# Four transformer blocks on one core: new due times and margins in the build-time plan, normalisations on VectorE or ScalarE, and the fp4 constant inside the rounding

## The chip, the cores and the metric

The kernel runs on one core of a Trainium2 chip. The core has five engines that work side by side, each with its own queue: TensorE (PE; its weight loads are shown apart as PEld), VectorE (DVE), ScalarE (ACT), GpSimd (POOL) and SyncE (SP), which here issues all DMAs. An engine works through its queue in order, and waits on semaphores for what other engines produce. The metric is device time in microseconds; lower is better.

## The reference

The input is 8 sequences of 1024 rows by 256 columns, in float32. Four blocks follow each other, each with a layer normalisation in front and a residual sum behind. Cut to what matters:

```python
x = x + L0_attn(layernorm(x))   # flow-style linear attention, 16 heads of 16; inside it, layer norms
                                # and a GELU network 256 -> 1024 -> 256
x = x + L0_ffn(layernorm(x))    # relu(x @ w1 + b1) @ w2 + b2, width 1024
x = x + L1_attn(layernorm(x))   # softmax(Q K^T / 16) V, one head, within a sequence
x = x + L1_ffn(layernorm(x))    # fp4: silu(xq @ wgq.T) * (xq @ wuq.T), then quantised again @ wdq.T

def fp4_quant_dequant(x):       # blocks of 16 columns
    scale = max(abs(block)) / 6
    return nearest_on_grid([0, .5, 1, 1.5, 2, 3, 4, 6], abs(x / scale)) * sign(x) * scale
```

The first attention needs running sums along the rows of a sequence (of k, of q, of both weighted), so that a group of rows depends on the group before it. The softmax attention needs all 1024 rows of a sequence at once. The fp4 weights are 704 by 256 (gate, up) and 256 by 704 (down), and are quantised in the kernel.

## The kernel before, in words

**Tiling.** Rows go in chunks of 128 (64 chunks: 8 sequences of 8). Four chunks make a group of 512 rows, so there are 16 groups, two to a sequence; `p` numbers them. Two chunks of a group are a half.

**Stages.** They are written as Python generators:

- `linear_group(p)` normalises the four chunks (`front`), and then `linear_span` makes q and k, the running sums (`prod`, by VectorE's scan), the head sums on TensorE (`hsum`, narrow matmuls of 32 columns), and the weights per row. The first group is done in two halves (`near`). Through `spread` a packed row of weights goes to DRAM and back, widened.
- `linear_chunk(p, i)` makes v, the masked scores `sc` within a chunk (narrow `kz` matmuls), adds the running state `kv_sum`, projects with `wo`, normalises, and turns the result `h` into the half `hT`.
- `dense()` (L1412) runs the two 256-1024-256 networks for each half: 8 first matmul pairs into `hidden`, and 8 second ones that add into `acc`, two steps behind (`LAG`). `load_weights` fetches their weights again for each half pair, 256 KB in a DMA, two buffers each. `norms_1` and `norms_2` take the results, with layer normalisations, and turn them (`nT`, `n2T`).
- `soft_chunk(cc)` (L1580) does the softmax attention of a chunk and its fp4 network: scores, `prob` by Exp, `prob` turned into `probT`, product with `vt`, a normalisation `n`, `fp4(n)`, `n` turned into `xqT`, gate and up matmuls, `hid`, `fp4(hid)`, `hid` turned into `hqT`, the down matmul.
- `fp4_weights` quantises and turns 18 pieces of weights once; `softmax_weights` makes one matrix of Wq and Wk.

**Turning.** [...] rows must be transposed at many places. `flip` (L660) has two ways: on TensorE (two 128x128 matmuls against `ident`, a PSUM bank, one ScalarE copy), or by DMA: POOL copies the 32-bit tile as two halves of 16 bits (`cut`), a DMA transposes it (`spun`), and ScalarE copies it together. The first way is taken if `near` is asked for, or if `plan.idle` finds no part that could take TensorE now: `IDLE = 1, 0.0` (L29) means "fewer than one part for TensorE is ready, looking 0.0 us ahead".

**The plan.** The order of all instructions is made at build time by `Plan.run` (L313). Each generator (a part) yields a need: an engine, tiles that must be done, buffers or banks that must be free, a condition, and perhaps a due time `at`, counted in groups. The planner keeps its own clock for each engine, from a table of costs in `took` (L167), and takes the part with the smallest key:

```python
wait = max(max(t) - now - (0.3 if stays or part[2] < 0.0 else 0.0), 0.0)
unripe = 0.0 if urgent else max(t[1] + self.RIPE[queue] - now, 0.0)
key = wait, unripe, queue == "tensor", not stays, part[2]
```

`now` is TensorE's planned time. `unripe` is a margin: operands should have been done for `RIPE` us before a step is placed. `part[2]` is the due time, which decides last. For other engines than TensorE a step counts as startable 0.5 us before its engine is free (L288). All five queues are pinned: an instruction is chained to the one before it on its engine, so that the order of the plan is the order on the chip. If the plan sees TensorE pause for over 1.6 us ahead of one of its steps, `fill` (L1734) puts dummy matmuls of `ident` by `ident` there, one for each 0.22 us.

**Normalisation** (`layernorm`, L637): VectorE takes mean and variance, POOL makes `ln_ve` and `ln_rstd`, VectorE computes (x - mean) * rstd in one instruction.

**fp4** (L723): after scaling to blocks, ScalarE squares into `c` (bf16), a VectorE instruction adds 2^22 * 4/3 to `c`, and `src + c - c` rounds `src` to a step that grows with its size; then the block scale is multiplied on.

Of the kernel before, what the change touches and what calls it, by code (L numbers as in the profile page):

```python
# [17 lines left out]
P = 128  # L18
# [9 lines left out]
W_FF = 2  # L28
IDLE = 1, 0.0  # L29
RES = 10  # L30
HALVES = 5
LAG = 2
QB = 16
# [36 lines left out]
class Plan:  # L70
# [8 lines left out]

    RIPE = {"tensor": 1.0, "vector": 0.5, "scalar": 0.5, "gpsimd": 0.0, "sync": 3.0}  # L80
    SETS = {AF.Gelu: 1, AF.Exp: 2, AF.Sigmoid: 3}
# [177 lines left out]
    @staticmethod  # L259
    def need(queue, tiles, banks=0, when=None, at=None, unused=(), fresh=None, tiled=False):  # L260


        return SimpleNamespace(
            queue=queue, tiles=tiles, banks=banks, when=when, at=at, unused=unused, fresh=fresh,
            tiled=tiled,
        )

    def pe(self, *tiles, **kw):
# [14 lines left out]
    def ready(self, need):  # L283


        if need.when is not None and not need.when():
            return None
        free = self.free.get(need.queue, 0.0) - (0.0 if need.queue == "tensor" else 0.5)  # L288
        times = [0.0]
        times += [self.done.get(x.tensor.name, 0.0) for x in need.tiles]  # L290
        times += [self.used.get(x.tensor.name, 0.0) for x in need.unused]
        if need.banks:
            times.append(self.banks_free(need.banks))
        if need.fresh is not None:
            times.append(self.buffer(need.fresh)[0])
        return None if None in times else (free, max(times))
# [81 lines left out]
def block_stack_kernel(ctx: ExitStack, tc: tile.TileContext, a: dict, out: bass.AP):  # L378
# [258 lines left out]
    def layernorm(kind, src):  # L637
        mean, rstd = ln_stats(src)
        dst = yield from fresh(kind, dve(rstd), "n")
        nc.vector.tensor_scalar(dst, src, mean, rstd, ALU.subtract, ALU.mult)  # L640
        return dst
# [18 lines left out]
    def flip(src, dst, tiles=None, last=None, near=False):  # L660

        if not near:
            yield plan.pool(src)
            near = plan.idle(*IDLE)
        if near:
            yield pe(src, banks=1)
            bank = turned([src[:, k, :] for k in range(2)])
            if last is not None:
                plan.drop(last)
            if tiles is not None:  # L670
                tiles.cut += 1
            yield act(bank)
            nc.scalar.copy(dst, bank)
            if tiles is not None:
                tiles.done += 1
            return
        cut = yield from fresh("cut", plan.pool(src))
        nc.gpsimd.tensor_copy(
            cut.rearrange("p (h k t) -> p h k t", h=2, k=2),
            src.bitcast(U16).rearrange("p k (t h) -> p h k t", h=2),  # L680
        )
        if last is not None:
            plan.drop(last)
        if tiles is not None:
            tiles.cut += 1
        spun = yield from fresh("spun", dma(cut))
        nc.sync.dma_start_transpose(out=spun.rearrange("p (b t) -> p b t", t=P), in_=cut)
        plan.drop(cut)
        yield act(spun)
        nc.scalar.copy(  # L690
            dst.bitcast(U16).rearrange("p k (t h) -> p k t h", h=2),
            spun.rearrange("p (h k t) -> p k t h", h=2, k=2),
        )
        plan.drop(spun)
        if tiles is not None:
            tiles.done += 1
# [26 lines left out]
    def fp4(src, width, rows=P, factor=1.0):  # L723
# [21 lines left out]
            blocks(src, width),  # L745
            factor * (1.0 - 2.0**-23),
            wide(rc, rows, nb),
# [6 lines left out]
        yield dve(c)  # L754
        nc.vector.tensor_scalar(c, c, 2.0**22 * 4.0 / 3.0, None, ALU.add)
        nc.vector.tensor_tensor(src, src, c, ALU.add)
        yield dve(src)
        nc.vector.tensor_tensor(src, src, c, ALU.subtract)
        plan.drop(tile_c)
# [4 lines left out]
    def fp4_weights():  # L764
# [15 lines left out]
        for i, (src, turns) in enumerate(pieces):  # L780
            for j in range(i, min(i + 3, len(pieces))):
                if j not in raws:
                    ahead = pieces[j][0]
                    raws[j] = (yield from fresh(
                        "soft",
                        dma(at=2.0 + 2.5 * i / len(pieces), when=lambda: count["stage"] == 4),
                        "w_raw",
# [5 lines left out]
            raw = raws.pop(i)  # L793
            at = 2.0 + 2.5 * i / len(pieces)
            yield dve(raw, at=at)
# [179 lines left out]
    def linear_group(p):  # L975
# [28 lines left out]
        fronts = set()  # L1004
        yield dve(at=p, when=lambda: count["v"] == p * G)
        n0T = two(kept([P, 2 * GT], "n0T", 1))
        for i in range(G):
            plan.start(front(i), p + 0.03 * i - (p == 0 and i < 2))
        tiles = SimpleNamespace(
# [18 lines left out]
    def linear_span(p, span, fronts, tiles):  # L1028
# [16 lines left out]
        def turn(n):  # L1045
# [4 lines left out]
        yield pe(  # L1050
            at=p + 0.1 + after,
            when=lambda: fronts >= set(span)
# [24 lines left out]
        for n, pair in enumerate(((2, 0), (3, 1))):  # L1077
            for b in pair:
                need = dve(cur[b], at=p + 0.15 + 0.08 * n + after, when=turn("flow"))
                prod = prods[(b + 2) % 4] = (yield from fresh("flow", need, "prod"))[:, :width]  # L1080
                yield from running(prod, cur[b], past["cur"], b, opens, closes)
# [5 lines left out]
        ran.add(("flows", span.stop))  # L1087
        yield pe(*prods, banks=1, tiled=True, at=p + 0.3 + after, when=lambda: "hsum" in late)
        bank = head_sums(prods, span)
# [11 lines left out]
        for n, pair in enumerate(((2, 0), (3, 1))):  # L1101
            for b in pair:
                w = weighted[b]
                need = dve(w, at=p + 0.35 + 0.08 * n + after, when=turn("scale"))
                if near:
# [10 lines left out]
            for b in pair:  # L1116
# [3 lines left out]
                )  # L1120
        yield pe(*prods, banks=1, tiled=True, at=p + 0.5 + after, when=lambda: "positions" in late)
        bank = head_sums(prods, span)
# [62 lines left out]
        )  # L1185
        plan.start(scaled(), p + 0.55 + after)
        for i in span:
            plan.start(linear_chunk(p, i, n0T, comp, qk), p + 0.55 + 0.03 * i + after)

    def linear_chunk(p, i, n0T, comp, qk):  # L1190

        s, g = divmod(p, NG)
        past, c = seqs[s]["past"], p * G + i
        at = p - (p == 0 and i < 2)
        here = slice(i * P, (i + 1) * P)
# [40 lines left out]
        for e in range(2):  # L1236
# [5 lines left out]
                qk[1],  # L1242
                at=at + 0.62 + 0.06 * i,
                when=lambda: i in groups[p]["scaled"]
# [51 lines left out]
        if not end:  # L1296
            k_at = at + 0.66 + 0.06 * i
            need = plan.pool(at=k_at, when=lambda: count["attended"] >= c - (p > 0))
# [78 lines left out]
        if by_act and i == G - 1:  # L1377
            plan.drop(later)
        yield pe(xo, banks=1, at=at + 0.7 + 0.06 * i, when=lambda: "chunk" in late)
        bank = mm_bank()  # L1380
        for k in range(2):
# [12 lines left out]
            h,  # L1394
            at=at + 0.74 + 0.06 * i,
            when=lambda: half_fits(p, "hT", i // 2) and count["dense"] >= p - 1,
# [15 lines left out]
    def dense():  # L1412
# [4 lines left out]
        def second():  # L1417
# [21 lines left out]
            if f == NF - 1:  # L1439
# [10 lines left out]
                for j in range(2):  # L1450
                    norms = (norms_1, norms_2)[b]
                    plan.start(
                        norms(p, 2 * half + j, acc[:, j * D : (j + 1) * D], taken),
                        p + 1 + (2 * b + half + 1) / 4,
                    )

        def load_weights(names, used, loaded, first):

            ws, n = [], 0
            for p in range(flows):  # L1460
                for name in names:
                    for f in 2 * list(range(0, NF, 2)):
                        yield dma(
                            at=p + 0.9 + (2 * n % 32 + (0 if first else LAG)) / 32,
                            when=lambda: n < W_FF + used[0] // 2 and count["stage"] >= 2,
# [20 lines left out]
        for p in range(flows):  # L1486
            for b, (kind, ba, func) in enumerate((("hT", b1, AF.Gelu), ("nT", fb1, AF.Relu))):
                for half in range(2):
# [3 lines left out]
                    for f in range(NF):  # L1492
                        yield pe(
                            at=p + 1 + (16 * b + 8 * half + f) / 32,
                            when=lambda: n_turned.get((kind, half)) == 2 and w_in and "dense" in late,
# [84 lines left out]
    def soft_chunk(cc):  # L1580
# [3 lines left out]
        n2T, vt = q["n2T"], q["vt"]  # L1584
        at = 3.5 + min(cc, B * NCH - 10) / 4
        yield pe(
# [47 lines left out]
        for kb in range(NG):  # L1634
            tp = yield from fresh("prob", plan.pool(prob[kb], at=at + 0.25), "probT")
            probT.append(tp.rearrange("p (k t) -> p k t", k=G))
            rows_kb = prob[kb].rearrange("p (k t) -> p k t", k=G)
            flips.append(
                flip_all([(rows_kb[:, j : j + 2], probT[kb][:, j : j + 2]) for j in (0, 2)], at + 0.25)
            )  # L1640
# [23 lines left out]
        yield from fp4(n, D)  # L1664
        xqT = two((yield from fresh("soft", plan.pool(n, at=at + 0.5), "xqT")))
        yield from flip(two(n), xqT, last=n)
# [30 lines left out]
        for half in range(2):  # L1697
            tq = yield from fresh("prob", plan.pool(hid, at=at + 0.75), "hqT")
            hqT.append(tq.rearrange("p (k t) -> p k t", k=4))
        for j in range(0, len(INTER_TILES), 2):  # L1700
            src = two(hid[:, j * P : (j + 2) * P])
            pairs.append((src, hqT[j // 4][:, j % 4 : j % 4 + 2]))
        flips_h = flip_all(pairs, at + 0.75)
        yield plan.pool(when=lambda: flips_h.cut == len(pairs))
# [20 lines left out]
    def softmax_and_fp4():  # L1725
        for cc in range(B * NCH):
            q = seqs[cc // NCH]
            yield dve(
                at=3.5 + min(cc, B * NCH - 10) / 4,
                when=lambda: q["normed"] == NCH and cc - count["out"] < (8 if plan.spare else 4) and "softmax" in weights and "ends" in late,  # L1730
            )
            plan.start(soft_chunk(cc), 3.5 + min(cc, B * NCH - 10) / 4)

# [54 lines left out]
```

## Time and profile before

| What | Before |
|---|---|
| median of 3 runs | 2533.13 us (2532.2 to 2544.2) |
| the profiled execution's own time | 2542.89 us |
| its span, first to last instruction | 2541.2 us |
| mean granted TensorE clock | 0.995 |
| DMA traffic | 305.54 MB, mean 120 GB/s |
| DMA transposes (spun) | 713 |
| table loads on ScalarE | 166, 213.0 us |
| the chain that ended last | PE 67%, DVE 17%, DMA 6%, ACT 5%, POOL 3%, issue 2% |

Almost every instruction is recorded through one helper, so all carry line 359: groups are told apart by their tiles, written out<-in. A float32 matmul appears as two records (passes), a transposition as one. The busy time of a matmul is modelled [...], so records overlap; the distance from start to start says how long TensorE is taken.

### The profile page before, as it was taken

The page shows a single profiled execution, that of the slowest core. Times are in us where ns is not written, and L with a number is a line of the kernel's source. Part 1 is how long each engine was busy: PE and PEld are TensorE (multiplying, and loading weights), DVE is VectorE, ACT ScalarE, POOL GpSimd, SP SyncE. Part 2 cuts the span into 40 slices and gives each one's busy share as a digit, 9 for nine tenths or more (in the row PEclk, how much of TensorE's full clock was granted, in tenths as well). Part 3 has the DMA queues.
Part 4 walks back from the last instruction along what each step waited for, and adds up shares of the span by engine and source line. Part 5 has one row for each costly group of instructions (what it writes and reads, how often), then busy time and mean ns, then how long its engine had stood idle before and what let it go on. Part 6 is the DMA issues. An engine that isn't in the chain of part 4 may idle for free.

```text
span 2541.2 us, 47871 instructions
## 1 busy us (share of the span) xinstructions
PE 2469.1 (97%) x16713; PEld 1919.0 (76%) x16713; DVE 1995.0 (79%) x4414; ACT 1376.0 (54%) x2842; POOL 1089.1 (43%) x1947
## 2 busy tenths in 40 slices
PE   8999999999999999999999999999999999999999
PEld 7777777777777777777777777777677777877767
DVE  6786778877868778797987868787788887866788
ACT  4544556465565554556455464645656455545463
POOL 2343445452534525444452544635345353534242
PEclk9999999999999999999999999999999999999999
DMA  3445465565546544555545455555454645545342
GB/s 88 99 135 138 114 153 117 133 135 125 123 118 146 120 116 110 134 132 122 144 108 138 107 127 131 128 133 118 106 141 116 154 99 126 123 110 131 69 87 53
DMA packets 600977, 305.54 MB, mean 120 GB/s; under 512 B 404384, under 2 KB 589216, under 8 KB 600736
## 3 DMA queue, kind: packets, MB, share of 16 engines
q1 hardware_dynamic: 600736, 302.48, 49.6%
q8 instruction: 132, 2.16, 0.4%
q14 instruction: 109, 0.89, 0.1%
HBM read 188.17 MB, written 20.71 MB: 82 GB/s over the span
## 4 chain that ended last, share of the span: by engine, by line
PE 67%; DVE 17%; DMA 6%; ACT 5%; POOL 3%; issue 2%; SPq 1%; DVEq 0%; POOLq 0%; ACTq 0%
PE bank L359 67%; DMA spun<-cut 4%; DVE hid L359 2%; DVE n L359 2%; ACT L359 2%; DVE prod L359 2%; DVE ln_st L359 1%; DVE u L359 1%; POOL ln_rstd L359 1%; DMA spread<-packed 1%; DVE sc L359 1%; SPq L359 1%; DVE res L359 1%; DVE mx L359 1%; DVE ln_mv L359 1%
## 5 line engine op out<-in xcount | busy, mean ns | idle before, releaser
L359 PE MATMUL bank<-half,w_in 128*128 128x256 f32 x2048 | 532.2, 383 | 13.9 <-ACT half L359 9.9
L359 PE MATMUL bank<-w_out,hidden 128*128 128x256 f32 x2048 | 534.2, 385 | 8.7 <-DMA w_out<-in_L_ffn_w_dram 7.5
L359 PEld LDWEIGHTS bank<-w_out,hidden 128*128 128x128 f32 x2048 | 376.8, 191 | 108.9 <-issue 52.6
L359 PEld LDWEIGHTS bank<-half,w_in 128*128 128x128 f32 x2048 | 386.0, 191 | 88.5 <-issue 19.8
L359 POOL TENSOR_SCALAR ln_ve<-ln_mv 128x1 f32<-128x1 f32 x384 | 95.9, 250 | 737.6 <-DVE ln_mv L359 723.3
L359 POOL TENSOR_TENSOR ln_rstd<-ln_ve,neghalf 128x1 f32<-128x1 f32 x384 | 236.4, 616 | 31.9
L359 PE MATMUL bank<-n2T,qT 128*128 128x512 f32 x512 | 242.2, 595 | 4.3 <-ACT qT L359 3.6
L359 PE MATMUL bank<-vt,probT 128*128 128x256 f32 x1024 | 231.9, 379 | 0.0
L359 ACT ACT_TABLE_LOAD x166 | 213.0, 1283 | 16.2 <-DVE nmax L359 11.3
L359 ACT ACTIVATE hidden<-bank,c_L_ffn_b 128x256 f32<-128x256 f32 x256 | 121.0, 473 | 183.8 <-PE bank L359 182.9
L359 POOL COPY cut<-prob 128x512 uint16<-128x512 uint16 x211 | 143.2, 702 | 176.3 <-ACT prob L359 124.6
L359 PEld LDWEIGHTS bank<-vt,probT 128*128 128x128 f32 x1024 | 194.0, 190 | 30.4 <-issue 3.1
L359 ACT COPY probT<-spun 128x512 uint16<-128x512 uint16 x241 | 158.6, 675 | 85.0 <-DMA spun<-cut 82.0
L359 ACT ACTIVATE hidden<-bank,c_L_attn_b 128x256 f32<-128x256 f32 x256 | 120.0, 470 | 146.1 <-PE bank L359 145.7
L359 POOL COPY cut<-n 128x512 uint16<-128x512 uint16 x200 | 138.5, 698 | 129.2 <-DVE n L359 108.2
L359 PE MATMUL bank<-wgT,xqT 128*128 128x352 f32 x512 | 174.9, 464 | 10.5 <-ACT xqT L359 9.8
L359 PE MATMUL bank<-wdT,hqT 128*128 128x256 f32 x768 | 176.5, 380 | 0.5 <-DVE v L359 0.5
L359 PE MATMUL bank<-wuT,xqT 128*128 128x352 f32 x512 | 172.3, 459 | 0.0
L359 PEld LDWEIGHTS bank<-wdT,hqT 128*128 128x128 f32 x768 | 145.1, 190 | 21.7 <-DVE v L359 0.9
L359 POOL COPY cut<-hid 128x512 uint16<-128x512 uint16 x158 | 108.3, 706 | 109.9 <-DVE hid L359 87.2
L359 PEld LDWEIGHTS bank<-n2T,qT 128*128 128x128 f32 x512 | 96.3, 190 | 76.5 <-issue 58.5
L359 ACT COPY hqT<-spun 128x512 uint16<-128x512 uint16 x173 | 114.2, 675 | 64.7 <-DMA spun<-cut 64.4
(240 smaller groups left out, 4783.2 us busy)
## 6 DMA issues: line engine op xcount, KB each, us to landing
w_in<-in_L_attn_W_dram SPq DMA_DIRECT2D x128, 256.0 KB
w_out<-in_L_attn_W_dram SPq DMA_DIRECT2D x128, 256.0 KB
w_in<-in_L_ffn_w_dram SPq DMA_DIRECT2D x128, 256.0 KB
w_out<-in_L_ffn_w_dram SPq DMA_DIRECT2D x128, 256.0 KB
spread<-packed SPq DMA_DIRECT2D x90, 256.0 KB
spun<-cut SPq DMA_TRANSPOSE x713
x<-in_L_attn_inputs_dram SPq DMA_DIRECT2D x64, 128.0 KB
xr<-in_L_attn_inputs_dram SPq DMA_DIRECT2D x64, 128.0 KB
```

Source lines behind the costliest of these rows:

```text
L359: ins = method(*args, **kw)
```

## The change

Six things are edited.

1. Due times and margins get names in one table `T`, with new values. The offsets within a group (`p + 0.15`, `p + 0.3`, ...) become entries of it; `lin` is 0.0 and adds nothing. The start of the softmax chunks stays at 3.5, their clamp near the end goes from 10 to 11 chunks. The `RIPE` margins change: TensorE 1.0 to 0.935, VectorE 0.5 to 0.744, ScalarE 0.5 to 0.298, POOL stays 0.0, SyncE 3.0 to 6.94. The 0.5 us of lead becomes 0.51. Weight loads are due 0.069 of a group later, dense steps 0.049 earlier.
2. `flip` looks 1.173 us ahead where it looked 0.0 ahead, so it takes TensorE only if no TensorE step becomes ready within that time.
3. `plan.either` lets a step have two engines; the planner takes the one that is free first in its own clock, with 0.745 us put on ScalarE.
4. `layernorm` uses it: POOL makes one more small tile, `ln_shift` = -mean * rstd, and the normalisation is either the VectorE instruction of before or a ScalarE `Identity` with scale `ln_rstd` and bias `ln_shift`. In the plan both wait for `ln_shift`; of the instructions only ScalarE's reads it. `layernorm_affine` stays as it is.
5. fp4: the addition of the constant to `c` is taken into the two passes after it, as three-operand instructions with the constant in float32; the sign of the first factor is turned to fit.
6. The fp4 weights: loading is let in from stage 3 on (before: at stage 4), due at 3.15 + 4.022 i/18 (before 2.0 + 2.5 i/18).

```diff
-IDLE = 1, 0.0
+T = dict(
+    span=-0.073, prods=0.117, pair=0.137, sums=0.05, weighted=0.269, sums2=0.303, chunk=0.625,
+    scores=0.819, turn_k=0.822, xo=0.419, turn_h=0.629, step=0.095, dense=-0.049, norm=0.528,
+    soft=3.5, soft1=0.277, soft2=0.575, soft3=0.75, fp4=3.15, fp4_over=4.022, tail=11,
+    weights=0.069, shy=0.745, ripe_t=0.935, ripe_v=0.744, ripe_s=0.298, ripe_g=0.0, ripe_d=6.94,
+    back=0.51, ahead=1.173, stage=3, lin=0.0,
+)
...
+    def either(self, queues, *tiles, **kw):
+        need = self.need(next(iter(queues)), tiles, **kw)
+        need.queues = queues
+        return need
...
-        free = self.free.get(need.queue, 0.0) - (0.0 if need.queue == "tensor" else 0.5)
+        if need.queues is not None:
+            need.queue = min(need.queues, key=lambda q: self.free.get(q, 0.0) + need.queues[q])
+        free = self.free.get(need.queue, 0.0) - (0.0 if need.queue == "tensor" else T["back"])
...
-        dst = yield from fresh(kind, dve(rstd), "n")
-        nc.vector.tensor_scalar(dst, src, mean, rstd, ALU.subtract, ALU.mult)
+        shift = small([P, 1], "ln_shift", 8)
+        nc.gpsimd.tensor_scalar(shift, mean, rstd, -1.0, ALU.mult, ALU.mult)
+        need = plan.either({"vector": 0.0, "scalar": T["shy"]}, shift)
+        dst = yield from fresh(kind, need, "n")
+        if need.queue == "vector":
+            nc.vector.tensor_scalar(dst, src, mean, rstd, ALU.subtract, ALU.mult)
+        else:
+            nc.scalar.activation(dst, src, AF.Identity, bias=shift, scale=rstd)
...
-            near = plan.idle(*IDLE)
+            near = plan.idle(1, T["ahead"])
...
-            factor * (1.0 - 2.0**-23),
+            -factor * (1.0 - 2.0**-23),
...
-        nc.vector.tensor_scalar(c, c, 2.0**22 * 4.0 / 3.0, None, ALU.add)
-        nc.vector.tensor_tensor(src, src, c, ALU.add)
+        k = 2.0**22 * 4.0 / 3.0
+        nc.vector.scalar_tensor_tensor(src, c, k, src, ALU.add, ALU.add)
         yield dve(src)
-        nc.vector.tensor_tensor(src, src, c, ALU.subtract)
+        nc.vector.scalar_tensor_tensor(src, c, k, src, ALU.add, ALU.subtract)
...
-                        dma(at=2.0 + 2.5 * i / len(pieces), when=lambda: count["stage"] == 4),
+                        dma(at=T["fp4"] + T["fp4_over"] * i / len(pieces), when=lambda: count["stage"] >= T["stage"]),
...
-            at = 2.0 + 2.5 * i / len(pieces)
+            at = T["fp4"] + T["fp4_over"] * i / len(pieces)
...
-                need = dve(cur[b], at=p + 0.15 + 0.08 * n + after, when=turn("flow"))
+                need = dve(cur[b], at=p + T["lin"] + T["prods"] + T["pair"] * n + after, when=turn("flow"))
...
-                at=at + 0.62 + 0.06 * i,
+                at=at + T["scores"] + T["step"] * i,
...
-                        p + 1 + (2 * b + half + 1) / 4,
+                        p + 1 + (2 * b + half) / 4 + T["norm"],
...
-                            at=p + 0.9 + (2 * n % 32 + (0 if first else LAG)) / 32,
+                            at=p + 0.9 + T["weights"] + (2 * n % 32 + (0 if first else LAG)) / 32,
```

The other due times are replaced in the same manner (`RIPE` likewise).

## The prediction

> **What bounds the kernel now.** I read the page first, then TensorE's waits, the busy time by stage, a stretch of the timeline, and last the groups. All sums below stand against the profiled execution: span 2541.2 us, 2542.9 us with the 1.7 us around it. The runs have a median of 2533.1 us (2532.2 to 2544.2), 9.8 us less, so I take what I find off the median too. That spread of 0.5% is also about what this measurement can tell from no change.
>
> From the page (busy us, share, instructions), and from the view of waits (us in total, times, longest):
>
> ```profile
> PE 2469.1 (97%) x16713; PEld 1919.0 (76%) x16713; DVE 1995.0 (79%) x4414; ACT 1376.0 (54%) x2842; POOL 1089.1 (43%) x1947
> ```
>
> ```profile
> PE bank L359 <- ACT half L359: 9.9, 6, 5.7
> PE bank L359 <- ACT xqT L359: 9.8, 9, 2.1
> PE bank L359 <- DMA w_out<-in_L_ffn_w_dram: 7.5, 2, 4.5
> ```
>
> TensorE is idle for 2541.2 - 2469.1 = 72 us, in waits that no single releaser dominates. By stage (columns: busy us of PE, PEld, DVE, ACT, POOL, granted clock, DMA share, GB/s):
>
> ```profile
> 0.00:340.00 340.00, 309.70 (x2651) 251.89 (x2652) 247.72 (x596) 159.21 (x378) 124.22 (x249) 0.98 0.44 116
> 340.00:2505.00 2165.00, 2127.56 (x13876) 1640.16 (x13875) 1721.48 (x3774) 1207.01 (x2446) 960.11 (x1691) 1.00 0.52 122
> 2505.00:2541.00 36.00, 31.86 (x189) 26.96 (x187) 25.80 (x45) 9.80 (x19) 4.79 (x7) 1.00 0.19 48
> ```
>
> Idle is 30 us in the start, 37 us over the long middle, 4 us at the end. No other engine is near full anywhere, so only TensorE's work and its gaps set the time. The timeline prices that work from start to start (columns: start, us, engine and tiles):
>
> ```profile
> 602.73 1.03 PE L359 MATMUL bank<-w_out,hidden 128*128 128x256 f32 x4
> 603.68 1.08 PE L359 MATMUL bank<-prod,hsum 128*32 128x128 f32 x32
> 604.70 1.13 PE L359 MATMUL bank<-half,w_in 128*128 128x256 f32 x4
> 605.66 1.05 PE L359 MATMUL bank<-n2T,wqk 128*128 128x128 f32 x8
> 606.55 1.03 PE L359 MATMUL bank<-w_out,hidden 128*128 128x256 f32 x4
> 607.42 1.03 PE L359 MATMUL bank<-half,w_in 128*128 128x256 f32 x4
> 608.28 0.38 PE L359 MATMUL bank<-ident,prob 128*128 128x128 f32 x2
> 608.50 1.03 PE L359 MATMUL bank<-w_out,hidden 128*128 128x256 f32 x4
> ```
>
> Four 256-column passes take 0.87 us (606.55 to 607.42), a transposed pair 0.22 us, 0.11 per pass. A narrow block costs about 0.09 us extra on entry (603.68 - 602.73 - 0.87) and 0.09 on leaving (605.66 - 604.70 - 0.87).
>
> [...] In us: the 4096 dense passes 887; 2560 more of 256 columns 554; 752 of 512, four in 1.72 us by the same view, 324; 1024 of 352, four in 1.18, 303; 512 of 128 57; narrow blocks with their switches 212 by their starts; some 25 of small ones. That is 2362 us that must be done. Dummies (412 x 0.11 = 45) and transposes (about 283 x 0.11 = 31) bring it to 2438. So at most some 180 us can go, most of it spread thin. [...]
>
> **The change, part by part.** The diff tells little, since the planner places everything anew; I count the instructions in both built programs.
>
> ```profile
> L359 PE MATMUL bank<-ident 128*128 128x128 f32 x412 | 53.3, 289 | 3.1 <-POOL ident masks.py:199 3.1
> L359 PE MATMUL bank<-ident,n 128*128 128x128 f32 x112 | 21.8, 279 | 3.1 <-DVE v L359 1.7 <-DVE n L359 1.2
> L359 DVE TENSOR_SCALAR n<-res,ln_mv,ln_rstd 128x256 f32<-128x256 f32 x128 | 64.0, 503 | 22.0 <-POOL ln_rstd L359 21.2
> L359 ACT ACTIVATE kz<-k,parity 128x256 f32<-128x256 f32 x128 | 57.0, 500 | 0.4
> L359 DVE TENSOR_SCALAR q_c<-q_c 128x704 bf16<-128x704 bf16 x64 | 25.3, 395 | 25.3 <-ACT q_c L359 24.8 <-ACT ahead L359 0.4
> L359 DVE TENSOR_TENSOR hid<-hid,q_c 128x704 f32<-128x704 f32 x116 | 107.0, 923 | 2.2
> L359 DVE SCALAR_TENSOR_TENSOR hid<-hid,x_r 128x704 f32<-128x704 f32 x58 | 55.2, 951 | 0.6
> L359 POOL TENSOR_SCALAR ln_ve<-ln_mv 128x1 f32<-128x1 f32 x384 | 95.9, 250 | 737.6 <-DVE ln_mv L359 723.3
> ```
>
> *TensorE, the path.* Transposes fall by 92 (n -46, hid -20, prob -12, k -10, h -6, flow +2): -92 x 0.11 = **-10 us**. Dummies fall from 206 to 200 instructions, two passes each: -12 x 0.11 = **-1 us**; but they move: 135 to 159 in the start (+5 us), 23 to 12 in the middle, 48 to 29 at the end. Entries into narrow blocks fall by 12: -12 x 0.18 = **-2 us**. All other matmuls are the same in number.
>
> *The 46 flips that leave TensorE* each become a POOL copy (0.70 us), a DMA transpose and a ScalarE copy of 0.675 in place of 0.371. POOL +32 us, ScalarE +14 us, SP 46 more issues. These lie beside TensorE. What they cost is delay: single pieces of 4 to 5 us stand in the chain under spun<-cut. Uncovered, 46 x 4 = 184 us; covered, nothing. The new order gives more cover at most places. Priced by the passes above, the TensorE work between producer and user at the lower quartile goes from 27 to 39 us (dense output to the next half), 27 to 33 (probT product to xqT), 17 to 20 (scores to probT product). It shrinks from 32 to 21 from the wo product to its half. I take nothing.
>
> *fp4.* 146 additions on VectorE go: 64 x 0.395 + 78 x 0.284 + 1 = -48 us. The two passes after them become three-operand ones; the nearest rows (951 against 923 for 704 columns, 458 against 524 for 256) say between +4 and -10 us: nothing. The negated factor is free.
>
> *Normalisations.* 117 of 256 move to ScalarE: VectorE -(71 x 0.503 + 16 x 0.482 + 30 x 0.495) = -58 us. On ScalarE I price them by kz, also 256 columns from SBUF: +117 x 0.50 = +58 us. [...] The rows show an even trade, and I take them. POOL gets 256 ln_shift at 0.25 us: +64 us. A moved one waits for ln_shift; directly behind it on ScalarE stand 23 times an activation hidden<-bank, for which TensorE waits, else mostly copies. Table loads fall by 38 (x 1.283 = -49 us) and their triggers by 18 (-4).
>
> Sums: VectorE 1995 - 107 = 1888, ScalarE 1376 + 58 + 14 - 53 = 1395, POOL 1089 + 64 + 32 = 1185. None becomes the bound.
>
> *Due times, margins, fp4 weights.* One unknown: what the new order makes of the 72 us idle and of the clock. The granted clock stands at half in five pieces of 3.4 to 6.8 us after the start, 20 us together, which cost 10. If every wait of the middle and a third of the start goes, and the clock with them, -57 us; if the start, which gets more dummies, and the middle grow by half, +34. I stay near the low side of the gain: a third of the middle, none of the start, -12, and a third of the clock's 10, **-3**. The ground is a VectorE with 107 us less to do and longer cover. What is late next is the start: the same chain of scans, head sums and first flips.
>
> Sum: -10 - 1 - 2 - 12 - 3 = -28, near 2513 us of span; off the median, about **2504 us**.
>
> **Rivals.**
> 1. *Only counted work goes.* Gaps merely change places: -13, 2520 us. For it: the waits are many and short; the start's dummies grow. Against: cover grows.
> 2. *The order drains most gaps.* -13 - 57 = -70, 2463 us. For it: VectorE is in many short waits. Against: the middle is 98% busy already.
> 3. *ScalarE's queue becomes the brake* (slower). A normalisation waits on POOL in front of hidden activations; DVE n<-ln_rstd waits of that kind take 38.0 us in 54 times, 0.70 each. If all 117 wait 0.70 and half of it reaches TensorE, +41, with the counted -13 net +28: 2561 us. It decides from about 0.22 us per normalisation reaching TensorE (26 us: 13 of counted gain and 13 to be called slower). Against: hidden has 7 us of TensorE cover at the lower quartile in both orders.
> 4. *The change does not do what it says:* excluded in counts, since the built programs differ as told.
>
> **Numbers.** Forecast (2483 to 2516) 0.50; rival 1 (2516 to 2545) 0.22; rival 2 0.17; rival 3 0.11. Faster by over 0.5% means under 2520.5: the first, rival 2 and under half of rival 1, 0.77; same 0.12; slower 0.11. The range of 8 in 10, with a tenth left out on each side, is 2468 to 2542.
>
> **What would show it.** Right: about 92 fewer records of bank<-ident,..., VectorE near 1890 us, ScalarE near 1395, POOL near 1185, TensorE's idle near 60 us with the middle under 30. Normalisations on ScalarE at 0.45 to 0.50 us. Wrong: TensorE waiting on ACT hidden or half (rival 3), on spun<-cut copies, or the start's idle well over 30 us.

## The result, and the profile after

The changed kernel takes 2498.99 us (median of 4 runs, 2495.58 to 2500.84). The kernel before took 2536.76 us beside it (4 runs, 2532.2 to 2544.2). The ratio is 0.985, with a 95% interval of 0.982 to 0.988: faster by 1.5%, or 38 us by the medians. The forecast was 2504 us against 2533.1, a ratio of 0.989 (its own sum of -28 us gives 2505).

The profiled execution took 2495.6 us with a span of 2493.9. From its page, busy time of the engines and the chain that ended last:

```profile
PE 2445.0 (98%) x16609; PEld 1910.6 (77%) x16609; DVE 1901.3 (76%) x4151; ACT 1392.5 (56%) x2903; POOL 1228.8 (49%) x2249
...
PE 80%; DVE 4%; POOL 1%; issue 1%; ACT 0%; DMA 0%; DVEq 0%; POOLq 0%; ACTq 0%
```

TensorE has 104 passes fewer, VectorE 94 us less to do, ScalarE 16 us and POOL 140 us more. The chain has become TensorE's own: its share went from 67% to 80%, VectorE's from 17% to 4%, and the DMAs' 6% are gone. TensorE's idle time is now 2493.9 - 2445.0 = 48.9 us, 23 less. Its largest waits are short again and have new names (us in total, times, longest):

```profile
PE bank L376 <- DMA w_out<-in_L_attn_W_dram: 6.3, 2, 4.7
PE bank L376 <- DVE w_raw L376: 4.8, 4, 2.0
PE bank L376 <- ACT half L376: 4.1, 8, 1.3
```

The waits for `half` shrank from 9.9 us to 4.1, those for `xqT` from 9.8 us to under 1. The busy time by stage (columns: length, then busy us and instructions of PE, PEld, DVE, ACT, POOL, then granted clock, DMA share, GB/s):

```profile
0.00:340.00 340.00, 305.83 (x2656) 250.26 (x2657) 237.47 (x559) 164.82 (x392) 126.30 (x267) 0.96 0.40 111
340.00:2455.00 2115.00, 2106.73 (x13787) 1634.53 (x13786) 1636.51 (x3547) 1214.28 (x2485) 1096.66 (x1976) 1.00 0.54 128
2455.00:2494.00 39.00, 32.42 (x168) 25.82 (x167) 27.37 (x47) 13.45 (x26) 5.87 (x7) 1.00 0.24 53
```

The middle over the same 2115 us in the kernel before:

```profile
340.00:2455.00 2115.00, 2077.56 (x13679) 1604.40 (x13678) 1676.78 (x3673) 1178.28 (x2388) 942.19 (x1661) 1.00 0.52 123
```

The middle's idle time fell from 2115 - 2077.6 = 37.4 us to 8.3, and 108 more matmul records fit into the same time. The start's went up, from 30.3 us to 34.2, and the last stretch's from 4.1 to 6.6. So the idle time that went lies wholly in the middle, where VectorE is busy for 77% of the time and no other engine but TensorE for more.

Three waits cost more than their length. In the kernel before, TensorE's granted clock stands at half for three stretches of 3.4 us in the middle (from 657.8, 1415.6 and 1719.4 us), each just behind a wait of TensorE (1.0, 3.0 and 4.5 us). The second one in the timeline, and as a stage:

```profile
1415.31 3.48 PE L359 MATMUL bank<-w_out,hidden 128*128 128x256 f32 x8 [2.98 <-DMA w_out<-in_L_ffn_w_dram]
```

```profile
1415.60:1419.00 3.40, 3.40 (x9) 2.69 (x8) 1.02 (x3) 0.20 (x1) 2.75 (x7) 0.50 0.24 46
```

The eight passes take 3.27 us from start to start (the next one starts at 1418.58), where 0.217 each would be 1.74. Other waits of 1.5 to 2.1 us in the same middle have no such stretch behind them. In after the middle has none; in the start it is the other way round, 13.7 us at half clock before and 23.9 after. The sum is 23.9 us in both.

The two profiled executions lie further apart than the medians, 47.3 us by their spans: 23 are idle time and 11 the 104 passes. About 12 more are, by an estimate from the distances from start to start, delays too short to show as idle behind a record's modelled end.

The changed work itself, from the groups (busy us, mean ns of one, then the idle time before and what ended it):

```profile
L376 ACT ACTIVATE n<-res,ln_shift,ln_rstd 128x256 f32<-128x256 f32 x71 | 42.5, 598 | 51.3 <-POOL ln_shift L376 50.9 <-DVE ln_st L376 0.2
L376 DVE TENSOR_SCALAR n<-res,ln_mv,ln_rstd 128x256 f32<-128x256 f32 x57 | 22.7, 405 | 5.9 <-POOL ln_rstd L376 5.7
L376 ACT ACTIVATE kz<-k,parity 128x256 f32<-128x256 f32 x128 | 57.1, 499 | 0.2
L376 POOL TENSOR_SCALAR ln_shift<-ln_mv,ln_rstd 128x1 f32<-128x1 f32 x256 | 85.1, 333 | 26.5
L376 DVE SCALAR_TENSOR_TENSOR hid<-q_c,hid 128x704 f32<-128x704 bf16 x116 | 107.8, 930 | 12.2 <-ACT q_c L376 11.3
```

A normalisation on ScalarE takes 0.60 us, 0.10 more than `kz`. It waits for `ln_shift` as forecast, 0.7 us each time (50.9 us for 71). The fp4 passes with three operands take 930 ns for 704 columns, where the two-operand pass took 923.

### The profile page after: what moved, and what is told of

It reads as the page before. It is cut to its first block, busy times and chain, and to the rows that moved or that the text cites. A ratio compares the mean times of both kernels' runs of the same rounds, so it can differ in the third digit from the quotient of the medians.

```text
span 2493.9 us, 47900 instructions
## 1 busy us (share of the span) xinstructions
PE 2445.0 (98%) x16609; PEld 1910.6 (77%) x16609; DVE 1901.3 (76%) x4151; ACT 1392.5 (56%) x2903; POOL 1228.8 (49%) x2249
## 4 chain that ended last, share of the span: by engine, by line
PE 80%; DVE 4%; POOL 1%; issue 1%; ACT 0%; DMA 0%; DVEq 0%; POOLq 0%; ACTq 0%
PE bank L376 80%; DVE hid L376 1%; DVE x_amax L376 0%; DVE k L376 0%; POOL cut L376 0%; DVE n L376 0%; POOL ln_rstd L376 0%; DVE q L376 0%; DVE x_r L376 0%; DVE ln_st L376 0%; DVE mx L376 0%; DVE x_s L376 0%; DMA spun<-cut 0%; DVE u L376 0%; DVE y L376 0%
## 5 line engine op out<-in xcount | busy, mean ns | idle before, releaser
L376 PE MATMUL bank<-w_out,hidden 128*128 128x256 f32 x2048 | 528.5, 385 | 10.1 <-DMA w_out<-in_L_attn_W_dram 6.3
L376 POOL TENSOR_SCALAR ln_ve<-ln_mv 128x1 f32<-128x1 f32 x384 | 105.1, 274 | 599.4 <-DVE ln_mv L376 580.1
L376 POOL COPY cut<-n 128x512 uint16<-128x512 uint16 x223 | 152.3, 692 | 120.3 <-DVE n L376 63.4
L376 POOL COPY cut<-hid 128x512 uint16<-128x512 uint16 x168 | 125.3, 773 | 132.2 <-DVE hid L376 124.8
L376 PEld LDWEIGHTS bank<-wuT,xqT 128*128 128x128 f32 x512 | 97.3, 190 | 54.2
```

Source lines behind the costliest of these rows:

```text
L376: ins = method(*args, **kw)
```

## The experiments

Four theories stood against each other. **A**: the new order alone makes the gain, and the relief of VectorE is idle time that nobody waits for. **B**: the relief makes it, in any order. **C**: the order and the relief only work together, since the values were chosen for a plan with these operations. **D**: every microsecond taken from VectorE has about the same price, whatever it was and in whatever order.

To change work without changing the order, some kernels let the planner count one instruction and issue another. `chained` issues an instruction at the end of an engine's queue without telling the planner; `plan.took` tells the planner without issuing. All medians are of 4 runs; the kernel before had 2537.7, 2537.8 and 2539.5 us beside the three sets of four. The times of after stand beside a before of 2536.8 us, so a difference from after can be off by up to 3 us for the set alone. "Middle" is TensorE's idle time from 340 to 2455 us, "start" that of the first 340.

### The new order with the old work

The order of after on TensorE, POOL and SyncE is kept. The 146 additions on VectorE are issued again (with 0.0), and the 117 moved normalisations run on VectorE, where the plan had counted them on ScalarE. These are not the places that a plan would have found for them in VectorE's queue.

```diff
-            nc.scalar.activation(dst, src, AF.Identity, bias=shift, scale=rstd)
+            chained("vector", "tensor_scalar", dst, src, mean, rstd, ALU.subtract, ALU.mult)
+            plan.took("scalar", "activation", (dst, src, AF.Identity), dict(bias=shift, scale=rstd))
...
         k = 2.0**22 * 4.0 / 3.0
+        chained("vector", "tensor_scalar", c, c, 0.0, None, ALU.add)
```

> The changed kernel with its order of instructions kept on TensorE, POOL, SyncE, but VectorE gets its old work back at the places of the new plan: the 146 fp4 additions are issued again (adding 0.0) and the 117 moved normalisations run on VectorE although the plan counts them on ScalarE. VectorE 1901 + 107 = about 2008 us busy, ScalarE 1393 - 70 = 1322. If the new order and its cover make the gain (theory A), 2499 to 2511 us and TensorE's idle in the middle stays under 20 us. If the relief of VectorE makes it (theory B), most of the gain goes: 2520 to 2535 us, with the middle's idle near 35 us.

Measured: 2522.3 us, ratio 0.993 (0.992 to 0.995). The middle by stage:

```profile
340.00:2455.00 2115.00, 2097.21 (x13758) 1621.53 (x13757) 1691.37 (x3725) 1155.64 (x2368) 1086.28 (x1959) 1.00 0.55 128
```

Its idle time is 17.8 us: two thirds of the way from 37.4 to 8.3, and under 20 as A had it. The time is where B had it. The new order alone is worth 15.4 us, about as much as the TensorE work that was counted off, 13 us; but some idle time went too (72.0 to 63.6 us in all), and the time at half clock grew from 23.9 to 42 us (a mean granted clock of 0.995 before and 0.992 here). The other 23.3 us come only once VectorE is relieved. A falls.

Since TensorE's queue is the same in both, the same pass can be looked up in both traces. How many us this kernel and three of the later ones start it behind after:

| at after's time | 350 | 1000 | 2350 | end |
|---|---|---|---|---|
| old work in the new order | 9.5 | 14.6 | 23.6 | 28.8 |
| only the additions back | 6.0 | 7.0 | 9.2 | 13.9 |
| only the normalisations back | 6.7 | 9.4 | 15.6 | 16.5 |
| all normalisations on ScalarE | 4.0 | 3.9 | 13.9 | 15.1 |

There is no one place of loss: a part is lost in the start, and the rest in small pieces all along. The traces are single executions, after's the fastest of its four (3.4 us under the median) and that of "only the normalisations back" the slowest (5.5 over), so the ends lie further apart than the medians.

### The old order without the additions

Before's order is kept, and only the 146 additions are gone.

```diff
-        nc.vector.tensor_scalar(c, c, 2.0**22 * 4.0 / 3.0, None, ALU.add)
-        nc.vector.tensor_tensor(src, src, c, ALU.add)
+        k = 2.0**22 * 4.0 / 3.0
+        plan.took("vector", "tensor_scalar", (c, c, k, None, ALU.add), {})
+        nc.vector.scalar_tensor_tensor(src, c, k, src, ALU.add, ALU.add)
```

> The kernel before with its order kept on every engine, but without the 146 fp4 additions on VectorE (constant inside the rounding; the plan still counts them). VectorE 1995 - 48 = 1947 us. Theory A: under 0.3% of gain, 2529 to 2537 us, since the gaps sit in the order. Theory B: 48 of the 107 us of relief are there, so near half of the 23 us of idle that went should go: about 2525 us.

Measured: 2527.5 us, ratio 0.995 (0.993 to 0.997).

```profile
340.00:2455.00 2115.00, 2087.68 (x13741) 1615.53 (x13741) 1651.32 (x3580) 1186.78 (x2409) 947.50 (x1672) 1.00 0.51 124
```

Middle idle falls from 37.4 to 27.3 us, and the time by 10.2, while VectorE's busy time on the page falls by 46 (1995.0 to 1949.4). So 0.22 us of time goes with each us of VectorE's work in the mean, in the old order too, though VectorE is busy for only 79% of the span.

### The new values alone, and the new operations alone

The first has before's `layernorm` and `fp4` with the new table `T`; the second the new operations with the values of before. Both are planned anew.

```diff
-    span=-0.073, prods=0.117, pair=0.137, sums=0.05, weighted=0.269, sums2=0.303, chunk=0.625,
+    span=0.1, prods=0.15, pair=0.08, sums=0.3, weighted=0.35, sums2=0.5, chunk=0.55,
...
-    back=0.51, ahead=1.173, stage=3, lin=0.0,
+    back=0.5, ahead=0.0, stage=4, lin=0.0,
```

> The new due times, margins, look-ahead and fp4-weight stage on the old operations (normalisations all on VectorE, the additions in), planned anew. Theory A: 2499 to 2518 us. Theory B: 2520 us or more. The built program has 262 dummies against 206 before and 200 after, 56 x 0.22 = 12 us more than before, so a third theory, that times and operations only fit each other together (C), says 2515 to 2540 us.

> The new operations (normalisation on either engine, constant inside the rounding) on the old due times and margins, planned anew. Theory A: no gain, 2528 to 2545 us. Theory B: 2505 to 2520 us. Theory C: like A.

Measured: the values alone 2528.3 us, ratio 0.996 (0.994 to 0.997); the operations alone 2566.9 us, ratio 1.011 (1.009 to 1.013). The middle of the second:

```profile
340.00:2455.00 2115.00, 2074.41 (x13702) 1606.42 (x13701) 1574.07 (x3410) 1189.81 (x2428) 1002.74 (x1869) 1.00 0.51 123
```

VectorE has 95 us less to do than before (1900.0 against 1995.0), and TensorE idles more (40.6 us). Over the whole span it has 10 us more of idle time, 98 more passes (11 us), and 41 us at half clock in place of 24 (8 us more; mean granted clock 0.992). The same relief that gained in a kept order loses 29 us when the planner sets the order anew with its old values. B falls as a rule for what the change does. C is left, but it was not yet clear how much of such a result is the operations and how much is any new order.

### Margins moved by next to nothing

The kernel before, with TensorE's margin 1.0 set to 0.98 and the lead 0.5 to 0.51; nothing else. The diff is written against before; in the built kernel both stand in the table `T` (`ripe_t=0.98`, `back=0.51`), and all its other values are those of before.

```diff
-    RIPE = {"tensor": 1.0, "vector": 0.5, "scalar": 0.5, "gpsimd": 0.0, "sync": 3.0}
+    RIPE = {"tensor": 0.98, "vector": 0.5, "scalar": 0.5, "gpsimd": 0.0, "sync": 3.0}
...
-        free = self.free.get(need.queue, 0.0) - (0.0 if need.queue == "tensor" else 0.5)
+        free = self.free.get(need.queue, 0.0) - (0.0 if need.queue == "tensor" else 0.51)
```

> The kernel before with two margins moved by next to nothing (TensorE's ripeness 1.0 to 0.98, the lead 0.5 to 0.51), planned anew. It tells the scatter of replanning. Had the plan no scatter, 2532 to 2542 us. The built program has 10 more dummies and 28 more transposes than before (about 5 us of TensorE), so with scatter 2540 to 2570 us; a time under 2525 would say that before was an unlucky plan and that any new plan gains.

Measured: 2570.7 us, ratio 1.013 (1.011 to 1.015).

```profile
340.00:2455.00 2115.00, 2069.86 (x13625) 1595.34 (x13624) 1641.49 (x3599) 1159.03 (x2352) 934.05 (x1632) 0.99 0.50 121
```

Two margins moved by a fiftieth cost 33 us, with the same operations. TensorE has only 28 transposes and 20 dummy passes more (48 x 0.11 = 5 us); 8 us are idle time, and 48 us at half clock in place of 24 (mean granted clock 0.991) make about 12. So the 29 us of the operations alone lie within what this one control shows a new order of the planner can do, and say nothing against the operations; nor do the 9 us of the values alone say much for the values. C is neither shown nor refuted.

### One half of the relief taken back at a time

After's order is kept again; first only the additions are back on VectorE, then only the normalisations. The edits are the two hunks of the first experiment.

> The changed kernel in its own order, with only the 146 fp4 additions issued again on VectorE (adding 0.0): +48 us of VectorE work. With both parts of the old work back the changed kernel lost 23 us of 2499. Theory D (load: each us of VectorE work costs about 0.27 us wherever it stands): +13 us, 2510 to 2514. Theory E (delay on chains: an addition stands in the fp4 chain, which has 20 us and more of cover, a normalisation stands ahead of the first flips and of the halves): under +6 us, 2499 to 2505, and the moved normalisations carry the rest.

> The changed kernel in its own order, with only the 117 moved normalisations run on VectorE again: VectorE +52 us, ScalarE -70 us. Theory D: +12 to +16 us, 2511 to 2515, so that the two parts add up to the 23. Theory E: +17 us or more, 2516 to 2523. If ScalarE's load costs as much as VectorE's, the relief of ScalarE pays it back and the time stays at 2494 to 2502.

Measured: 2508.6 us, ratio 0.989 (0.987 to 0.990), with the additions back; 2506.5 us, ratio 0.988 (0.986 to 0.990), with the normalisations back. That is 9.6 us for 40 us of VectorE's busy time (1941.2 against 1901.3), and 7.5 us for 41 (1942.2): 0.24 and 0.18 us per us. The additions are worth the same as in the old order (10.2). Together the two were worth 23.3, 6 more than their sum. On average D holds so far.

By place it does not. The added instructions of the first kernel by stage (length, busy us and number on VectorE, granted clock, DMA share, GB/s):

```profile
0.00:350.00 350.00, 5.67 (x18) 0.96 0.40 110
350.00:1000.00 650.00, 9.81 (x33) 1.00 0.56 133
1000.00:2350.00 1350.00, 26.12 (x76) 1.00 0.56 130
2350.00:2508.00 158.00, 5.72 (x19) 0.99 0.33 70
```

Against the table of passes above, the 18 of the start, all for the fp4 weights, lie beside 6.0 us of lag (of which the clock makes up to 1.7, by an estimate of half of one stretch of 3.4 us), the 109 between 350 and 2350 us beside 3.2, and the 19 of the end beside 4.7. That is about 1 us per us in the start and 0.1 in the middle; the 0.24 is a mean over such stages.

Two things are mixed here. An added instruction fills VectorE's queue, and it also stands in the chain of the value that it works on. Some of the loss may be of the first kind: in the kernel with all the old work TensorE waits 2.1 us, in 3 times, for `scale` of the linear attention, which uses no value of the fp4 network, and for which it did not wait in after. How much is of either kind was not measured, since no run gave VectorE work that nobody waits for.

### More work for ScalarE

After's order is kept, and 139 times, behind each normalisation that stayed on VectorE, ScalarE gets an `Identity` of 128x256 on a tile that nobody reads.

```diff
             nc.vector.tensor_scalar(dst, src, mean, rstd, ALU.subtract, ALU.mult)
+            chained("scalar", "activation", scratch, scratch, AF.Identity)
```

> The changed kernel in its own order, with 139 more ScalarE instructions of 128x256 on a scratch tile that nobody waits for, one behind each normalisation that stayed on VectorE, at 0.5 to 0.6 us each: ScalarE +70 to +83 us. If load in any in-order queue costs 0.27 us per us, +19 to +22 us, 2518 to 2521. If ScalarE has room (56% busy), under +8 us, 2499 to 2507.

Measured: 2501.3 us, ratio 0.985 (0.983 to 0.988): 2.3 us more than after, with ranges that overlap. The added tile (duration in ns, least, median, most), and the middle:

```profile
L644 ACT ACTIVATE scratch<-scratch x139: 399/413/438, 7.3 to 2446.3; 128x256 f32<-128x256 f32 x139
```

```profile
340.00:2455.00 2115.00, 2107.25 (x13815) 1633.94 (x13814) 1631.57 (x3541) 1250.07 (x2611) 1092.74 (x1970) 1.00 0.55 129
```

The middle's idle time is 7.7 us, as in after. 139 x 0.413 = 57 us of extra work on ScalarE cost next to nothing where nobody waits for its result. So the 117 normalisations' own time on ScalarE is hardly what the move has to pay.

### All normalisations on ScalarE

After's order is kept, and the 139 others also go to ScalarE, at the places that the plan had for them on VectorE.

```diff
-            nc.vector.tensor_scalar(dst, src, mean, rstd, ALU.subtract, ALU.mult)
+            chained("scalar", "activation", dst, src, AF.Identity, bias=shift, scale=rstd)
+            plan.took("vector", "tensor_scalar", (dst, src, mean, rstd, ALU.subtract, ALU.mult), {})
```

> The changed kernel in its own order, with the other 139 normalisations too on ScalarE, at the places the plan gave them on VectorE: VectorE -59 us, ScalarE +83 us at 0.60 each. Theory D (each us of VectorE costs 0.15 to 0.27, ScalarE nothing): 2483 to 2490 us. Theory F (VectorE's load costs only where TensorE has gaps, and the changed kernel has 8 us of idle left in its middle): 2492 to 2500 us. If waits for ln_shift at the head of ScalarE's queue hold up hidden and the flips' copies: 2503 us or more.

Measured: 2510.6 us, ratio 0.989 (0.987 to 0.990), 11.6 us slower than after (10 by the two ratios). The page and the middle:

```profile
PE 2450.5 (98%) x16609; PEld 1912.1 (76%) x16609; DVE 1842.9 (73%) x4012; ACT 1458.0 (58%) x3042; POOL 1220.8 (49%) x2249
```

```profile
340.00:2455.00 2115.00, 2099.87 (x13770) 1627.07 (x13769) 1575.72 (x3397) 1266.54 (x2598) 1085.09 (x1966) 1.00 0.54 128
```

VectorE has 58 us less to do than in after, which by D should have gained some 12 us; TensorE idles 15.1 us in the middle where it idled 8.3. D falls as a rule to extrapolate by. A stretch of the timeline shows the way of the loss (start, us, engine, tiles, idle before and what ended it):

```profile
1088.51 0.59 ACT L644 ACTIVATE n<-rows,ln_shift,ln_rstd 128x256 f32<-128x256 f32 x1
...
1089.14 0.42 DVE L376 TENSOR_REDUCE x_amax<-n 128x16 f32<-128x256 f32 x1 [3.27 <-ACT n L644]
...
1091.75 0.42 ACT L376 ACTIVATE q_c<-n 128x256 bf16<-128x256 f32 x1 [2.64 <-DVE n L376]
...
1092.94 0.63 ACT L376 ACTIVATE qT<-bank,bqk 128x128 f32<-128x128 f32 x2
...
1093.37 1.95 PE L376 MATMUL bank<-n2T,qT 128*128 128x512 f32 x2 [1.98 <-ACT qT L376]
```

The normalisation stands behind an Exp (`prob`) in ScalarE's queue. VectorE waits 3.27 us for it, and comes late to `n`. Next in ScalarE's queue is `q_c`, which waits 2.64 us for `n`; behind it stand another normalisation, `hid`, `ahead` and `qT`. TensorE's passes for `qT` end at 1091.40, and `qT` starts at 1092.94. TensorE, which needs `qT`, idles 1.98 us, and the two passes shown take 1.95 us behind that; ten microseconds later (from 1103.99) four such passes take 1.88. Two views of waits show that this is no single case (us, times, longest):

```profile
DVE x_amax L376 <- ACT n L644: 68.1, 39, 3.7
ACT q_c L376 <- DVE n L376: 52.2, 38, 4.1
```

The second was 29.8 us in 26 times in after, and TensorE's waits for `qT` went from 2.3 to 8.8 us. This is the brake of the forecast's rival 3, ScalarE's queue, but by another wait: `q_c` for VectorE, and not a normalisation for `ln_shift` (19.0 us in 24 times for the 139) ahead of `hidden` (TensorE waits 0.2 us for it). These 139 were put where the plan had not placed them, which may be why it happens here.

### The transposes put back

After's order is kept, and 92 transposes of `ident` into a bank that is overwritten behind them are added, two in each of 46 chunks, ahead of the `wv` product.

```diff
+        if s * NCH + g * G + i < 46:
+            for k in range(2):
+                chained("tensor", "transpose", bank[:, k * P : (k + 1) * P], ident, ident)
```

> The changed kernel in its own order, with 92 more 128x128 transposes of a constant on TensorE, two ahead of the wv product in 46 of the 64 chunks, into a bank that the product then overwrites: they put back the TensorE time of the flips that left, without any wait. By the sum's own term +10 us (92 x 0.11), 2508 to 2510 us. If TensorE has slack there that hides them, under +4 us.

Measured: 2509.1 us, ratio 0.988 (0.987 to 0.990): 10.1 us more than after by the medians, 0.11 for each, and 8.6 by the two ratios. These 92 passes on TensorE are paid in full, or nearly.

### Values chosen anew, and costs corrected

The first moves ten values of `T` (fifteen, says the expectation) to ones for which the plan's own clock ends earlier. The second first corrects the planner's costs by what the profile shows (0.12 us more for an activation with scale and bias per row, 0.25 to 0.30 for POOL's one-column instructions where it had 0.22), and then chooses values in the same manner.

```diff
-    span=-0.073, prods=0.117, pair=0.137, sums=0.05, weighted=0.269, sums2=0.303, chunk=0.625,
+    span=-0.073, prods=0.117, pair=0.137, sums=0.05, weighted=0.373, sums2=0.31, chunk=0.625,
...
-    back=0.51, ahead=1.173, stage=3, lin=0.0,
+    back=0.51, ahead=1.027, stage=3, lin=0.0,
```

> The changed kernel with fifteen due times and margins moved a little further (weighted 0.269 to 0.373, xo unchanged, ahead 1.173 to 1.027, shy 0.745 to 0.857, TensorE's ripeness 0.935 to 0.895 and others), chosen by the plan's own clock: 6 fewer transposes, 3 fewer dummies. If the plan's clock orders plans rightly at this distance, 2480 to 2492 us; if its choice is lost in scatter, 2495 to 2515 us.

> The changed kernel with the planner told what the trace shows (a ScalarE instruction with scale and bias per row costs 0.12 us more, POOL's small instructions 0.25 to 0.30 us), and due times and margins chosen anew under these costs by the plan's own clock: 8 fewer transposes, 12 more dummies, 9 more entries into narrow blocks. If truer costs make truer cover: 2485 to 2497 us; scatter: 2497 to 2520 us.

Measured: 2493.6 us, ratio 0.982 (0.981 to 0.984), and 2498.9 us, ratio 0.984 (0.983 to 0.986). The middle of the first:

```profile
340.00:2455.00 2115.00, 2110.40 (x13820) 1639.01 (x13819) 1643.06 (x3564) 1205.90 (x2472) 1088.67 (x1984) 1.00 0.54 129
```

It is the lowest median of all and beats the kernel before, but its interval overlaps that of after (0.982 to 0.988), so it is not shown to be faster than after. The middle has 4.6 us of idle time left; the start has 37.9. Truer costs, with values chosen under them, did not bring more: 2498.9 is after's time.

## Why the prediction was right

The direction, the bound and the counted parts held; of the 38 us, 29 were forecast. That it came within 10 us owes something to luck: counted in the same way, the kernel with two moved margins has 5 us more of TensorE work, and it took 33 us longer. By the forecast's own steps:

1. **TensorE bounds the kernel, by its own work and its gaps.** Right. Its chain went to 80%, and 92 transposes put back cost 9 to 10 us, where the sum had 10. The weight loads' share of the span was 76% and is 77%, at a time 1.5% shorter; with 4.6 to 8.3 us left idle in a middle of 2115, that share did not tell what was left to be won.
2. **Narrow blocks, -2 us.** Their time by the starts went from 212.5 to 209.8 us, with the waits inside them, and the entries fell by 11. Dummies moved to the start, and a little further than counted (135 to 165 before 340 us in the traces, 159 in the forecast).
3. **Idle time, -12 us.** This is the term that was mis-sized. The middle gave up 29 us (37.4 to 8.3), not a third of 37. The start took 4 us more instead of none, and the end 2.5. The forecast named the right ground, "a VectorE with 107 us less to do and longer cover", but gave it no price of its own. The order without the relief comes to the counted 13 us and hardly more (2522.3 us against rival 1's 2520); the relief in that order makes 23.3 us.
4. **The clock, -3 us.** It did not come as a sum. The forecast counted five pieces, 20 us together; the trace has six, 23.9 us, three of them in the middle. After has five, also 23.9 us, all in the first 340 us. At half speed that is some 5 us won in the middle and 5 lost in the start.
5. **fp4, -48 us on VectorE, three-operand passes for nothing.** Right in kind: with the additions back VectorE has 40 us more, and the passes' durations are nearly as before (930 ns against 923 for `hid`; the pass with the negated factor has a median of 884 in both). Worth 10 us of time in either order, where the forecast had it inside the third.
6. **Normalisations, an even trade of 0.50 us.** Off on both sides. On ScalarE they take 0.60 us, 12 us more in all, which is hidden, if the run with the added `Identity` is a guide. Those left on VectorE got shorter in the mean (503 to 405 ns for `res`; the medians are 409 and 406, so fewer are drawn out), and taking the 117 back adds 41 us to VectorE's busy time, not 58.
7. **The busy times.** VectorE 1901 against 1888, ScalarE 1393 against 1395. POOL 1229 against 1185, because `ln_shift` takes 0.33 us and not 0.25, and `cut` of `hid` 0.77. TensorE waits directly for POOL only 4.8 us in after, 3.1 of them for `ident` at the very beginning.
8. **46 more DMA turns, nothing.** No wait for one of them stands among TensorE's largest, and DMAs left the chain (6% to 0%). It was not tried by itself.
9. **Rival 3.** Its wait is there, 0.7 us per normalisation on ScalarE, but TensorE's waits on `hidden` did not come (1.3 us before, 0.2 after), and TensorE's waits for `half` fell (9.9 to 4.1). With placements that the plan did not know, ScalarE's queue cost some 10 us, by the wait of `q_c`.
10. **The start is what is late next.** Right: 34.2 of the 48.9 us of idle time, all the half-speed stretches, and the 165 dummies besides.

What stays open: why two margins moved by a fiftieth cost 33 us, that is, which early choice of the planner sets the rest; how much of VectorE's price is its full queue and how much the longer chains; and what either half of the relief would bring with an order planned for it alone.

## What to carry to other kernels

An engine that is busy for three quarters of the time and off the bound can still have a price, here 0.2 us per us in the mean, and for the additions about 1 in the start and 0.1 in the middle. Queues that pass its lateness on, as ScalarE's did where `q_c` waited 2.64 us ahead of `qT`, are the likely reason, but this was not tried by itself. Keep the order fixed and change the work to measure that price, stage by stage. An order made by this greedy planner was a draw (two margins moved by a fiftieth cost 33 us): run the old kernel with a margin moved by nothing before a difference between two planned orders is put down to an operation. Work put on a less busy engine cost little here for its own time (57 us on ScalarE: 2.3 us), and more for its place in the queue where others wait behind it (the 139 normalisations: 10 to 12 us).

## What the runs showed of the hardware

- An activation on ScalarE of 128x256 takes 413 ns as an `Identity` with constants (`scratch`), 499 as a `Copy` with a scale per row (`kz`), and 598 as an `Identity` with a scale and a bias per row (`n`): 86 ns more, and another 99.
- ScalarE's records overlap. The 139 added instructions of 57 us raise its busy time on the page by 40 (1392.5 to 1432.8), while the other groups keep their sums; with 139 x 0.597 = 83 us of normalisations added it rose by 65.5. So about 0.12 us of each lies beside a neighbour, and by mean durations the 139 would have filled ScalarE's queue by 17 us more than they did.
- TensorE's busy time was not the same for the same passes: in after's order 16,609 records make 2445.0 us with the new work and 2458.7 with the old, 13.7 us of the 28.5 between the spans. TensorE's clock stands at half for 23.9 and 42 us in them, which by an estimate (half of the 18 us more, less what of it was idle) makes some 8 of the 13.7; what makes the rest was not shown.
- In the half-clock stretch at 1415.6 us a pass of 256 columns starts 0.427 us after the one before it, where it was 0.217 four microseconds earlier. All three such stretches in the middle of the kernel before stand behind a wait of TensorE.
